# Householder steps in two unequal column blocks, with the side matmuls spread anew

## The chip, the cores and the metric

The kernel runs on one core of a Trainium2 chip. The metric is the device time of one execution in microseconds, the median of the runs. The core has a matrix engine (TensorE, "PE" in the profile, with its weight loads listed as "PEld"), a vector engine (VectorE, "DVE"), a scalar engine (ScalarE, "ACT"), a general engine (GpSimd, "POOL") and DMA queues, of which this kernel uses mainly the one of SyncE ("SP"). Each engine works through its own instructions in order and waits on semaphores for the others.

## The reference

Input `x` is 8 sequences of 512 tokens with 576 features, with one conditioning vector per sequence. Two layers follow one another.

The first rotates part of each token. A matrix `P` (576 x 64) gives an orthonormal basis by a QR factorization, and each sequence gets its own rotation, the exponential of a skew matrix:

```python
U, _ = jnp.linalg.qr(P)                       # 576 x 64
R = expm(A)                                   # A: 64 x 64 skew, from silu(cond) @ W.T + b
z = jnp.einsum('btn,nd->btd', x, U)
x_rot = x + jnp.einsum('btd,nd->btn', jnp.einsum('btd,bde->bte', z, R) - z, U)
```

The second is a transformer block whose shifts, scales and gates come from `silu(cond) @ ada_w + ada_b`. Its attention is over the 16 heads of one token, not over tokens, and is followed by a gelu MLP of width 2304:

```python
x = x + gate_msa * attention(modulate(layernorm(x), shift_msa, scale_msa))
x = x + gate_mlp * mlp(modulate(layernorm(x), shift_mlp, scale_mlp))
```

All is float32.

## The kernel before

The kernel has two parts. A preparation computes the basis, the eight exponentials and the modulations; the main part then runs the block for 16 units of 256 tokens. The change lies in the preparation alone.

**The factorization.** `P` lies in SBUF as `m`: 128 partitions, five row chunks (`NK`), 64 columns (`R`). It is factored by 64 Householder steps, each a call of `qr_step(j, ...)`. In step j:

- TensorE copies row j to all partitions (`rp`, L274) and sums the column products over the partitions with a matrix of ones (`dp`, L282): entry j of `dp` is the squared norm of column j, the others are the inner products with it.
- VectorE takes the sign (`sg`, L291), zeroes the entry of row j in each column's place on the diagonal (`m<-m,off`, L292), and makes the reflected row (`row`, L295). ScalarE takes the root (`nrm`, L298).
- VectorE makes the coefficients `w` (L320) and the divisor `den` and its reciprocal `r` (L323, L335).
- VectorE updates the columns to the right: an outer product `up` (L327), then `m<-up,r,m` (L337), both in two halves of the columns.
- `column_products(j + 1)` makes the products of the next column with all (`pr`, L263) and sums them over the five chunks (`t`, L268). Step j + 1 begins with these.
- `finish` notes the diagonal's value (`av`, L306) and the column's largest entry (`vmax`, L307) and makes what must still be subtracted on the diagonal (`dg`, L310); the returned function subtracts it during the next step (L311).

With fewer than 16 columns left there is one block instead of two halves.

**Beside it.** TensorE has time between `dp` of one step and `rp` of the next. The generator `beside()` fills it: the main loop calls it once after each step from step 2 on, and what it issues stands in TensorE's queue behind that step's `dp` and ahead of the next `rp`. It does four things in turn:

- `skew_entries`: 8 groups of 5 matmuls ("pieces", L405), the entries of the skew matrices; then `skew_rows` sends them through DRAM into `au`.
- `modulations`: 9 groups of 5 matmuls against `ada_w` (L364; a piece here too), each group followed by a ScalarE copy and a load of another block of weights, and four groups followed by a set of small transposing matmuls, `modulation` (L375).
- the series of `expm`: 7 products of 64 x 64 blocks (L429) with additions on GpSimd (L462 to L489), spread over 13 calls.
- 19 squarings: two such products each (`pe` and `pf`), a ScalarE copy of each (L511) and a GpSimd addition for each (L513) that the next squaring reads.

`paced(n, ...)` hands out n pieces a call. In the kernel before, the skew pieces come four a call in steps 4 to 13, the modulations three a call from step 14 on and beside the series (steps 18 to 30), and the squarings in steps 31 to 49 with no other pieces. What is left runs afterwards.

The order of TensorE, VectorE, ScalarE and GpSimd in this part is the order in which the code issues (`manual_schedule`). The order of the loads on SP's queue is made by a planner. Loads for the main part go into memory that the preparation has used and wait until it is free: the first of them (L1048) waits for the last matmul against `ada_w`.

After the last step a serial tail (L574 to L703) forms the triangular factor's inverse by doubling and the matrices `u`, `ut` and `gz`, with which the main part begins.

## Time and profile before

| | us |
|---|---|
| median of 3 runs | 2158.01 |
| lowest and highest of them | 2157.17, 7304.47 |
| the profiled execution, its own time | 2156.77 |
| its span in the profile | 2155.1 |
| start of `sg` in step 0 and in step 63 | 5.87, 213.13 |
| busy over the span: PE, PEld, DVE, ACT, POOL | 2051.7, 1621.1, 1818.1, 432.9, 730.3 |
| mean granted TensorE clock | 0.96 |

The span is the time from the first to the last instruction that the profiler saw; the execution's own time also holds some 1.7 us around it. The highest of the three runs lies far off the other two, and the median is not moved by it. "Granted clock" is the TensorE clock as a share of full speed. A matmul of float32 values appears as two instructions, so a "piece" is two matmul records. A step j is counted from its `sg` to the next one.

### The profile page before, as it was taken

How to read it: one execution, taken by the hardware profiler on the slowest of the kernel's cores; microseconds unless marked ns; L12 is line 12 of the kernel's file. 1: busy time of each engine (PE TensorE's matmuls, PEld its weight loads, DVE VectorE, ACT ScalarE, POOL GpSimd, SP SyncE). 2: the span in 40 equal slices, each digit the busy share in tenths (PEclk: the TensorE clock that was granted, in tenths of full speed). 3: DMA queues.
4: the chain of work that ended last, by engine and by line, in shares of the span. 5: the costliest groups of instructions: out<-in, count | busy, mean ns of one | idle time of the engine just before them, and what ended most of it. 6: DMA issues, size and time to landing. Idle time of an engine off the chain costs nothing.

```text
span 2155.1 us, 28246 instructions
## 1 busy us (share of the span) xinstructions
PE 2051.7 (95%) x10109; PEld 1621.1 (75%) x10109; DVE 1818.1 (84%) x2548; ACT 432.9 (20%) x1040; POOL 730.3 (34%) x959
## 2 busy tenths in 40 slices
PE   5996898999999999999999999999999999998998
PEld 3476666777878878887878787888878787776777
DVE  8898499799997988979797979798997999989821
ACT  2232222221211221222121121121121211111210
POOL 2331153241523333333333243323333434343322
PEclk9855799999999999999999999999999999999999
DMA  8202256375757666575748484756657676665564
GB/s 278 87 2 75 82 189 176 116 227 167 216 192 205 210 185 213 170 236 161 249 137 270 127 266 147 223 194 195 221 177 222 194 226 166 205 188 189 168 193 139
DMA packets 251456, 392.44 MB, mean 182 GB/s; under 512 B 86926, under 2 KB 139099, under 8 KB 251316
## 3 DMA queue, kind: packets, MB, share of 16 engines
q1 hardware_dynamic: 225396, 364.09, 54.9%
q10 hardware_dynamic: 25920, 26.55, 3.6%
q8 instruction: 80, 1.31, 0.2%
q14 instruction: 60, 0.49, 0.1%
HBM read 331.63 MB, written 58.94 MB: 181 GB/s over the span
## 4 chain that ended last, share of the span: by engine, by line
PE 75%; DVE 16%; issue 3%; POOL 2%; DMA 2%; ACT 2%; ACTq 0%; SPq 0%; POOLq 0%; DVEq 0%
PE fc L1001 25%; PE qkvp L821 15%; PE fc L1075 9%; PE fc L1080 6%; PE pj L957 5%; DVE sc L866 3%; PE fc L1077 3%; PE p L1106 2%; DVE qk L859 2%; PE ada L364 1%; PE rot L762 1%; PE zps L751 1%; DVE att L894 1%; DVE pv L887 1%; PE dp L282 1%
## 5 line engine op out<-in xcount | busy, mean ns | idle before, releaser
L1001 PE MATMUL fc<-h2T,w 128*128 128x256 f32 x2304 | 519.0, 381 | 3.4 <-ACT h2T L977 2.3
L821 PE MATMUL qkvp<-wqkv,hT 128*128 128x288 f32 (+1 forms) x1920 | 484.4, 409 | 7.5 <-ACT qs L832 5.3
L1001 PEld LDWEIGHTS fc<-h2T,w 128*128 128x128 f32 x2304 | 433.6, 191 | 70.9 <-ACT h2T L977 9.5
L821 PEld LDWEIGHTS qkvp<-wqkv,hT 128*128 128x128 f32 (+1 forms) x1920 | 363.0, 191 | 110.0 <-ACT qs L832 7.1
L859 DVE TENSOR_TENSOR qk<-qkv 128x2304 f32<-128x2304 f32 x128 | 336.7, 2631 | 4.2 <-ACT qkv L829 2.0
L887 DVE TENSOR_TENSOR pv<-sc,qkv 128x2304 f32<-128x2304 f32 x128 | 333.5, 2606 | 2.7
L894 DVE TENSOR_REDUCE att<-pv 128x144 f32<-128x2304 f32 x128 | 326.0, 2547 | 3.1
L866 DVE TENSOR_REDUCE sc<-qk 128x64 f32<-128x2304 f32 x128 | 326.2, 2548 | 2.5
L1100 POOL TENSOR_TENSOR s<-gt 128x128 f32<-128x128 f32 x144 | 88.9, 619 | 453.3 <-ACT gt L1022 453.3
L1022 ACT ACTIVATE gt<-fc,b 128x256 f32<-128x256 f32 x288 | 118.8, 471 | 610.1 <-PE fc L1001 575.2
L1075 PE MATMUL fc<-wq,gt 128*128 128x288 f32 x576 | 170.8, 417 | 9.9 <-ACT gt L1022 6.7
L1080 PEld LDWEIGHTS fc<-wt,ss 128*128 128x128 f32 x1152 | 161.2, 191 | 15.3
L1080 PE MATMUL fc<-wt,ss 128*128 128x144 f32 x1152 | 165.1, 287 | 0.0
L1033 POOL TENSOR_TENSOR x<-x,mt 128x288 f32<-128x288 f32 x64 | 71.6, 1120 | 227.3 <-DVE mt L1032 227.3
L832 ACT COPY qs<-qkvp 128x288 f32<-128x288 f32 x180 | 71.5, 397 | 378.4 <-PE qkvp L821 337.9
L1097 POOL TENSOR_TENSOR ss<-gt 128x128 f32<-128x128 f32 x144 | 116.9, 812 | 69.6 <-PE fc L1080 68.0
L1099 POOL TENSOR_TENSOR ss<-gt,ss 128x128 f32<-128x128 f32 x144 | 133.0, 924 | 10.0
L1075 PEld LDWEIGHTS fc<-wq,gt 128*128 128x128 f32 x576 | 99.4, 190 | 44.4 <-issue 15.6
L957 PE MATMUL pj<-w2q_p,aT 128*128 128x288 f32 x384 | 104.0, 406 | 2.9 <-DVE u L1137 1.6
L146 POOL TENSOR_TENSOR rstd_m<-rstd_m,mhalf 128x1 f32<-128x1 f32 x32 | 26.7, 835 | 222.1 <-DVE rstd_m L145 222.1
L1075 PE MATMUL fc<-wt,gt 128*128 128x288 f32 x288 | 93.9, 408 | 0.0
L1077 PE MATMUL fc<-wq,ss 128*128 128x288 f32 x288 | 93.9, 408 | 0.0
(265 smaller groups left out, 2379.9 us busy)
## 6 DMA issues: line engine op xcount, KB each, us to landing
w<-in_fc_w SPq DMA_DIRECT2D x288, 256.0 KB, 5.0
wq<-in_fc_q SPq DMA_DIRECT2D x144, 432.0 KB, 4.3
wt<-comb_d SPq DMA_DIRECT2D x144, 432.0 KB, 5.6
tok<-qs ACTq DMA_DIRECT2D x180, 144.0 KB, 1.8
qkv<-tok SPq DMA_DIRECT2D x30, 864.0 KB, 4.6
w2q_p<-in_proj_w SPq DMA_DIRECT2D x32, 432.0 KB, 4.0
xT<-in_x_t SPq DMA_DIRECT2D x16, 640.0 KB, 4.9
w1t<-in_fc_t SPq DMA_DIRECT2D x80, 128.0 KB, 4.4
```

Source lines behind the costliest of these rows:

```text
L821: nc.tensor.matmul(ps, lhsT=hT[0:k, c, i * 128 : (i + 1) * 128], rhs=wqkv[0:k, c, cols], start=c == 0, stop=c == NK - 1,)
L859: nc.vector.tensor_tensor(pr, q[:, c * HC : (c + 1) * HC].unsqueeze(2).to_broadcast([128, HC, H, DH]), k.unsqueeze(1).to_broadcast([128, H ...
L866: nc.vector.tensor_reduce(sc[t][:, c * HC : (c + 1) * HC, :], pr, AX.X, ALU.add)
L887: nc.vector.tensor_tensor(pr, sc[t][:, c * HC : (c + 1) * HC, :].unsqueeze(2).to_broadcast([128, HC, DH, H]), v.unsqueeze(1).to_broadcast( ...
L894: nc.vector.tensor_reduce(att[:, c * HC : (c + 1) * HC, :], pr, AX.X, ALU.add)
L957: nc.tensor.matmul(ps, lhsT=aT[0:k, c, :], rhs=w, start=c == 0, stop=c == NK - 1)
L1001: nc.tensor.matmul(bank[:, k], lhsT=lhs, rhs=h2T[rows, c, 0 : NU * 128], start=start, stop=stop, skip_group_check=True)
L1022: nc.scalar.activation(gt[:, k].rearrange("p t s -> p (t s)"), bank[:, k], AF.Gelu, bias=b1[:, 2 * g + k : 2 * g + k + 1])
L1075: nc.tensor.matmul(p[k], lhsT=whole[k][0], rhs=whole[k][1], start=g == 0, stop=stop)
L1077: nc.tensor.matmul(p[2], lhsT=whole[2][0], rhs=whole[2][1], start=g == 0, stop=stop)
L1080: nc.tensor.matmul(bank[:, side], lhsT=lhs, rhs=rhs[:, n * QUARTER : (n + 1) * QUARTER], start=False, stop=stop, skip_group_check=True,)
L1099: nc.gpsimd.tensor_tensor(ss[:, 2], gt[:, 1, 0], ss[:, 1], ALU.subtract)
```

## The change

The columns are no longer halved. `split(lo)` puts the first quarter of those left in one block and the rest in another (still one block below 16). The two blocks have sums, products and `dp` tiles of their own, and the order within a step becomes: both outer products, `r`, the update of the quarter, `vmax`, the products of the next column with the quarter, the update of the rest, the sums of the quarter, the products and sums of the rest. `w` is made block by block. `av` and, while there are two blocks, `den` are made on ScalarE (`den` as `av` times `nrm`). The signs and diagonal values of all steps are kept in `sgs` and `avs`, and the diagonal is corrected once, after the last step, instead of in every step.

Beside it, the skew pieces come three a call (steps 4 to 16, and one more in 17), the modulation pieces three a call in steps 17 to 21 and two a call beside the series (steps 22 to 34), and none beside the squarings, which are steps 35 to 53. The rest comes one a call from step 54.

```diff
@@ -243,32 +243,33 @@
         vmax = prep.tile([128, R], F32, tag="vmax", name="vmax")
-        def halves(lo):
-            n = R - lo
-            if n < 16:
-                return [(lo, R)]
-            return [(lo, lo + n // 2), (lo + n // 2, R)]
+        avs = prep.tile([128, R], F32, tag="avs", name="avs")
+        sgs = prep.tile([128, R], F32, tag="sgs", name="sgs")
+        def split(lo):
+            first = lo + (R - lo) // 4
+            return [(lo, R)] if R - lo < 16 else [(lo, first), (first, R)]
         def wide(n):
             return [128, NK, n]
-        def column_products(j):
-            t = qrs.tile([128, R], F32, tag="t", name=f"t_{j}")
-            prods = []
-            for h, (a, b) in enumerate(halves(j)):
-                pr = qrs.tile(wide(R), F32, tag=f"pr{h}", name=f"pr_{j}_{h}", bufs=1)
-                nc.vector.tensor_tensor(
-                    pr[:, :, a:b], m[:, :, a:b], m[:, :, j : j + 1].to_broadcast(wide(b - a)), ALU.mult
-                )
-                prods.append(pr)
-            for pr, (a, b) in zip(prods, halves(j)):
-                nc.vector.tensor_reduce(t[:, a:b], pr[:, :, a:b].rearrange("p c i -> p i c"), AX.X, ALU.add)
+        def product(j, k, a, b):
+            pr = qrs.tile(wide(R), F32, tag=f"pr{k}", name=f"pr_{j}_{k}", bufs=1)
+            nc.vector.tensor_tensor(pr[:, :, a:b], m[:, :, a:b], m[:, :, j : j + 1].to_broadcast(wide(b - a)), ALU.mult)
+            return pr
+        def summed(j, k, a, b, pr):
+            t = qrs.tile([128, R], F32, tag=f"t{k}", name=f"t_{j}_{k}")
+            nc.vector.tensor_reduce(t[:, a:b], pr[:, :, a:b].rearrange("p c i -> p i c"), AX.X, ALU.add)
             return t
-        def qr_step(j, t, done):
+        def qr_step(j, ts):
             rp = ps_qr.tile([128, R], F32, tag="rp", name=f"rp_{j}")
             nc.tensor.matmul(
@@ -278,66 +279,75 @@
                 start=True,
                 stop=True,
             )
-            dp = ps_qr.tile([128, R], F32, tag="dp", name=f"dp_{j}")
-            nc.tensor.matmul(dp[:, j:R], lhsT=ones, rhs=t[:, j:R], start=True, stop=True)
-            def small(tag):
-                return qrs.tile([128, 1], F32, tag=tag, name=f"{tag}_{j}")
+            dps = []
+            for k, (t, (a, b)) in enumerate(zip(ts, split(j))):
+                dp = ps_qr.tile([128, R], F32, tag=f"dp{k}", name=f"dp_{j}_{k}")
+                nc.tensor.matmul(dp[:, a:b], lhsT=ones, rhs=t[:, a:b], start=True, stop=True)
+                dps.append(dp)
+            def small(tag, n=1):
+                return qrs.tile([128, n], F32, tag=tag, name=f"{tag}_{j}")
             n = R - j
-            row, sg, nsg, nrm, av = (small(x) if x != "row" else None for x in ("row", "sg", "nsg", "nrm", "av"))
-            row = qrs.tile([128, R], F32, tag="row", name=f"row_{j}")
+            row, nrm, den, r = small("row", R), small("nrm"), small("den"), small("r")
+            sg, av = sgs[:, j : j + 1], avs[:, j : j + 1]
             nc.vector.tensor_scalar(sg, rp[:, j : j + 1], 0.0, -2.0, ALU.is_ge, ALU.mult)
+            nc.vector.scalar_tensor_tensor(
+                row[:, j:R], sg.to_broadcast([128, n]), 1.0, rp[:, j:R], ALU.add, ALU.mult
+            )
             nc.vector.tensor_tensor(
                 m[:, 0, j:R], m[:, 0, j:R], off[:, j : j + 1].to_broadcast([128, n]), ALU.mult
             )
-            nc.vector.scalar_tensor_tensor(
-                row[:, j:R], sg.to_broadcast([128, n]), 1.0, rp[:, j:R], ALU.add, ALU.mult
-            )
-            nc.scalar.activation(nrm, dp[:, j : j + 1], AF.Sqrt, bias=tiny)
-            nc.scalar.activation(nsg, sg, AF.Identity, bias=ones[:, 0:1])
-            if done:
-                done()
-            def finish():
-                dg = small("dg")
-                nc.vector.tensor_scalar(av, nrm, row[:, j : j + 1], None, ALU.subtract)
+            nc.scalar.activation(nrm, dps[0][:, j : j + 1], AF.Sqrt, bias=tiny)
+            nc.scalar.activation(av, row[:, j : j + 1], AF.Identity, bias=nrm, scale=-1.0)
+            def largest():
                 nc.vector.tensor_reduce(
                     vmax[:, j : j + 1], m[:, :, j], AX.X, ALU.max, apply_absolute_value=True
                 )
-                nc.vector.tensor_scalar(dg, ident[:, j : j + 1], av, nsg, ALU.mult, ALU.mult)
-                return lambda: nc.vector.tensor_tensor(
-                    m[:, 0, j : j + 1], m[:, 0, j : j + 1], dg, ALU.subtract
-                )
+            cols = split(j + 1)
+            if len(cols) == 1:
+                largest()
             if j + 1 == R:
-                return None, finish()
-            w = qrs.tile([128, R], F32, tag="w", name=f"w_{j}")
-            den, r = small("den"), small("r")
-            nc.vector.scalar_tensor_tensor(
-                w[:, j + 1 : R], row[:, j + 1 : R], nrm, dp[:, j + 1 : R], ALU.mult, ALU.subtract
-            )
-            nc.vector.tensor_scalar(den, nrm, row[:, j : j + 1], nrm, ALU.subtract, ALU.mult)
-            outer = []
-            for h, (a, b) in enumerate(halves(j + 1)):
-                up = qrs.tile(wide(R), F32, tag=f"up{h}", name=f"up_{j}_{h}", bufs=1)
+                return None
+            if len(cols) == 1:
+                nc.vector.tensor_scalar(den, nrm, row[:, j : j + 1], nrm, ALU.subtract, ALU.mult)
+            else:
+                nc.scalar.activation(den, av, AF.Identity, scale=nrm)
+            w = small("w", R)
+            for dp, (a, b) in zip(dps, split(j)):
+                a = max(a, j + 1)
+                if a < b:
+                    nc.vector.scalar_tensor_tensor(w[:, a:b], row[:, a:b], nrm, dp[:, a:b], ALU.mult, ALU.subtract)
+            def outer(k, a, b):
+                up = qrs.tile(wide(R), F32, tag=f"up{k}", name=f"up_{j}_{k}", bufs=1)
                 nc.vector.tensor_tensor(
                     up[:, :, a:b],
                     m[:, :, j : j + 1].to_broadcast(wide(b - a)),
                     w[:, a:b].unsqueeze(1).to_broadcast(wide(b - a)),
                     ALU.mult,
                 )
-                outer.append(up)
-                if h == 0:
-                    nc.vector.reciprocal(r, den)
-            for up, (a, b) in zip(outer, halves(j + 1)):
-                nc.vector.scalar_tensor_tensor(
-                    m[:, :, a:b], up[:, :, a:b], r, m[:, :, a:b], ALU.mult, ALU.add
-                )
-            return column_products(j + 1), finish()
+                return up
+            def update(up, a, b):
+                nc.vector.scalar_tensor_tensor(m[:, :, a:b], up[:, :, a:b], r, m[:, :, a:b], ALU.mult, ALU.add)
+            ups = [outer(k, *ab) for k, ab in enumerate(cols)]
+            nc.vector.reciprocal(r, den)
+            update(ups[0], *cols[0])
+            if len(cols) == 2:
+                largest()
+            pr = product(j + 1, 0, *cols[0])
+            if len(cols) == 2:
+                update(ups[1], *cols[1])
+            ts = [summed(j + 1, 0, *cols[0], pr)]
+            if len(cols) == 2:
+                ts.append(summed(j + 1, 1, *cols[1], product(j + 1, 1, *cols[1])))
+            return ts
         def paced(n, parts):
@@ -528,14 +538,15 @@
         def beside():
             yield
             yield
-            yield from paced(4, [skew_entries(g) for g in range(8)])
+            yield from paced(3, [skew_entries(g) for g in range(8)])
             skew_rows()
-            rest = paced(3, [modulations()])
-            for _ in range(4):
-                next(rest)
+            rest = modulations()
+            for _ in range(5):
+                for _ in range(3):
+                    next(rest)
                 yield
             for free in expm(*eyes):
-                if free:
+                for _ in range(2 if free else 0):
                     next(rest, None)
                 yield
             for _ in rest:
@@ -551,9 +562,9 @@
         first_xt = xin.tile([128, D], F32, tag="xt", name="xt_0_0", bufs=2)
         eyes = identities()
         side = beside()
-        t, done = column_products(0), None
+        ts = [summed(0, k, a, b, product(0, k, a, b)) for k, (a, b) in enumerate(split(0))]
         for j in range(R):
-            t, done = qr_step(j, t, done)
+            ts = qr_step(j, ts)
             if j > 1:
                 next(side, None)
             if j == 30:
@@ -569,7 +580,10 @@
         if True:
-            done()
+            dg = prep.tile([128, R], F32, tag="dg", name="dg")
+            nc.vector.scalar_tensor_tensor(dg, sgs, 1.0, avs, ALU.add, ALU.mult)
+            nc.vector.tensor_tensor(dg, dg, ident[:, 0:R], ALU.mult)
+            nc.vector.tensor_tensor(m[:, 0, :], m[:, 0, :], dg, ALU.subtract)
             below = ps_ex.tile([R, 1], F32, tag="ex", name="below")
             nc.tensor.matmul(below, lhsT=vmax, rhs=ones[:, 0:1], start=True, stop=True)
             vv = ps_qr.tile([R, R], F32, tag="rp", name="vv")
@@ -618,7 +632,7 @@
                 nc.scalar.copy(vt[:, c * 128 : c * 128 + rows], ps[:, 0:rows])
             vx_chunk(0)
             for c, s in enumerate(LEVELS[1:], 1):
-                p1 = ps_qr.tile([R, R], F32, tag="dp", name=f"p1_{s}")
+                p1 = ps_qr.tile([R, R], F32, tag="dp0", name=f"p1_{s}")
                 nc.tensor.matmul(p1, lhsT=ls[s], rhs=x_, start=True, stop=True)
                 p1s = qrs.tile([R, R], F32, tag="p1s", name=f"p1s_{s}")
                 nc.vector.tensor_copy(p1s, p1)
@@ -663,7 +677,7 @@
             first_zT = prep.tile([R, 128], F32, tag="first_zT", name="first_zT")
             g0 = back(0)
-            zps = ps_qr.tile([R, 128], F32, tag="dp", name="first_z")
+            zps = ps_qr.tile([R, 128], F32, tag="dp0", name="first_z")
             nc.tensor.matmul(zps, lhsT=sneg[:, 0], rhs=vxs, start=True, stop=False)
             nc.tensor.matmul(zps, lhsT=ident[0:R, 0:R], rhs=first_xT[0:R, 0, 0:128], start=False, stop=True)
             nc.scalar.copy(gz[0:R, 0:HALF], g0)
```

## Prediction, made before the changed kernel was run

> **What bounds the kernel now.** I read the chain of waits first, then the factorization step by step.
>
> ```profile
> PE 75%; DVE 16%; issue 3%; POOL 2%; DMA 2%; ACT 2%; ACTq 0%; SPq 0%; POOLq 0%; DVEq 0%
> ```
>
> After 244 us TensorE sets the end and the change touches nothing there, so what the first 214 us gain or lose arrives whole at the end. Next the busy times by stretch, cut at the instants at which a step's `sg` (L291) starts: steps 4-16, 17-21, 22-34, 35-53, 54-62 (steps 0-3 took 5.87 to 21.70; the tail runs from 213.13 to 243.9). Columns: stretch, us; busy (count) of PE, PEld, DVE, ACT, POOL; clock; DMA.
>
> ```profile
> 21.70:66.28 44.58, 36.23 (x152) 15.85 (x151) 42.77 (x236) 8.96 (x35) 0.00 (x0) 1.00 0.67 224
> 66.28:87.77 21.49, 21.05 (x110) 9.28 (x110) 16.83 (x92) 5.27 (x20) 1.57 (x2) 0.76 0.32 92
> 87.77:137.97 50.20, 45.19 (x326) 25.57 (x322) 42.97 (x235) 12.99 (x48) 24.56 (x34) 0.73 0.10 33
> 137.97:191.77 53.80, 49.12 (x544) 44.32 (x543) 51.64 (x320) 19.66 (x68) 20.87 (x30) 0.50 0.14 46
> 191.77:213.13 21.36, 9.93 (x38) 8.93 (x37) 18.17 (x127) 3.98 (x18) 0.00 (x0) 0.50 0.20 75
> ```
>
> VectorE is full in steps 4-16 (3.43 us each) at full clock. From step 18 the clock comes and goes and PE is as full; through the squarings it is at half and both are full. So this is a VectorE chain with a TensorE load tuned to fit beside it. One VectorE step, the end of step 16 (start, duration):
>
> ```profile
> 63.57 0.26 DVE L320 SCALAR_TENSOR_TENSOR w<-row,nrm,dp 128x47 f32<-128x47 f32 x1
> 63.74 0.27 DVE L323 TENSOR_SCALAR den<-nrm,row 128x1 f32<-128x1 f32 x1
> 63.93 0.27 DVE L327 TENSOR_TENSOR up<-m,w 128x115 f32<-128x115 f32 x1
> ...
> 65.77 0.21 DVE L306 TENSOR_SCALAR av<-nrm,row 128x1 f32<-128x1 f32 x1
> 65.89 0.16 DVE L307 TENSOR_REDUCE vmax<-m 128x1 f32<-128x5 f32 x1
> 66.09 0.27 DVE L310 TENSOR_SCALAR dg<-ident,av,nsg 128x1 f32<-128x1 f32 x1
> 66.28 0.15 DVE L291 TENSOR_SCALAR sg<-rp 128x1 f32<-128x1 f32 x1
> ```
>
> An independent instruction starts some 0.09 us before its forerunner ends; a dependent one some 0.03 us after. And what TensorE pays, at half, full and half clock:
>
> ```profile
> 22.01 3.53 PE L405 MATMUL skew<-wr,sc 128*8 128x252 f32 x8
> 26.05 0.81 PE L405 MATMUL skew<-wr,sc 65*8 65x252 f32 x3
> ...
> 119.29 0.64 PE L274 MATMUL rp<-m,ident 128*128 128x34 f32 x2
> 119.73 0.62 PE L282 MATMUL dp<-t,ones 128*128 128x34 f32 x2
> 120.28 1.45 PE L364 MATMUL ada<-aw,sc 128*8 128x384 f32 x2
> ```
>
> A skew piece (two instructions) costs 3.53/4 = 0.88 us at half clock and 0.47 at full; an `ada` piece 1.29 and 0.65. The starts give `rp` 0.39-0.44, `dp` to the next work 0.55; at full clock (25.47, 25.73, 26.05) about 0.22 and 0.36.
>
> **The change, part by part.**
>
> *VectorE.* Gone per step: `av` 0.12, `dg` 0.18, the diagonal subtraction about 0.12, `den` 0.18 (intervals): -0.60, while there are two blocks. Added: a second `w` +0.17; `row` right behind `sg` and `r` right before its use +0.11; the sum of the large block right behind its product (end + 0.03 instead of overlapped) +0.12. Net about -0.2 to -0.35; I take -0.30. Below 16 columns `den` moves ahead of `w`, both behind `nrm`, and what was removed lay in the wait for `dp` there (206.0 to 206.8): 0, at worst +0.03 a step.
>
> *ScalarE* takes `av` and `den`: `row` ends 0.4 after `sg`, two activations of 0.28 end near 1.05, and `r` starts near 1.15. Hidden; if late, 0.1 a step.
>
> *TensorE* gets a third small product a step: `dp0` between `rp` and `dp1`. Before has no such triple. Floor 0 (where PE waits for VectorE anyway), ceiling a whole `rp` to `dp` spacing: 0.22 at full, 0.39 at half clock; I take the ceiling wherever PE is full. `dp1` keeps the place of `dp`, and only `w1` waits for it.
>
> *The side work.* Skew pieces go three a step (steps 4-16) instead of four (4-13), then 15 `ada` pieces in steps 17-21, two a step beside the series (22-34, four steps later), none beside the squarings (35-53), the last ten one a step from 54. The reload of the skew rows took 10.4 us (step 14 to 66.98); now it has five steps, at least 15 us: hidden. Weight loads on SP's queue waited for the last `ada` product (released at 183.4) and landed by about 196; that product now comes in step 63. Then they still have the 30 us tail for some 11 us of transfer: 0, at worst their 11 us.
>
> *What a step then costs.* At full clock VectorE leads: 3.43 - 0.30 = 3.13. At half clock PE leads: 0.39 + 0.39 + 0.56 + 3 x 0.88 = 3.98. So the clock decides, not the VectorE count.
>
> *The clock.* In before it changes on a grid of 3.41 us. At half, windows with side products in some 0.82 or more of them (22.0-25.5, 69.9-73.3, 100.7-104.1) were followed by full clock; 117.8-121.2 with 0.69 (products as above, `rp`/`dp` counted by their columns) was not. At full, four skew pieces with `rp` and `dp` (1.87 + 0.2 of 3.41 = 0.61) kept it; 66.6-70.0 with about 0.40 lost it. Three pieces: at full, one burst of 1.40 + 0.2 to 0.65 of other work = 0.47 to 0.60; at half, 0.72 to 0.85. Both lie inside the open gaps. I take two thirds half clock.
>
> A page of the Trainium skill speaks here: "TensorE: Matmul & The Clock Gate", section "HAM oscillation — how this bites in real kernels", gives as the rule for a full clock that PE must have no idle gap above some 3.4 us. By that rule PE, which never idles so long from step 4 on, stays at full everywhere, and the sum would be about -25 (every step at its VectorE time: -4, -6, -8, -5 in the four middle stretches, -2 elsewhere): 2133. The rows differ: 0.50 throughout 137.97:191.77 with PE busy 49.12 of 53.80. I go by the rows.
>
> Sum, against each stretch of before:
> - steps 0-3, no side work: 4 x -0.30 = -1.2.
> - steps 4-16: two thirds at 3.98, one third at 3.13 = 3.70 x 13 = 48.1 against 44.6: +3.5. (All full: 40.7, -3.9. All half: 51.7, +7.1.)
> - steps 17-21: three `ada` pieces at half are 3.87 us on end, more than a window, so the clock returns after two steps of 1.34 + 3.87 = 5.2; three of 3.1 and about 0.8 for a `mod` piece: 20.5 against 21.5: -1. (All full 15.5, -6; all half 27.8, +6.)
> - steps 22-34 at half: 13 x 1.34 + 22 x 1.29 + 2 x 1.8 (`mod`) + 7 x 0.98 (products of the series) = 56.3; at full VectorE's 3.0 to 3.2 beside the POOL operations, about 42. Two thirds half: 51.5 against 50.2: +1.5.
> - steps 35-53:
>
> ```profile
> 158.81 1.12 PE L429 MATMUL pf<-ex_f,ex_e 64*64 64x64 f32 x16
> 159.72 1.06 PE L429 MATMUL pe<-ex_e,ex_f 64*64 64x64 f32 x16
> 160.71 0.61 PE L274 MATMUL rp<-m,ident 128*128 128x21 f32 x2
> 161.18 0.59 PE L282 MATMUL dp<-t,ones 128*128 128x21 f32 x2
> 161.72 0.59 PE L429 MATMUL pe<-ex_e,ex_f 64*64 64x64 f32 x6
> ```
>
> PE has no gap: 2.91 a step. With `dp0` it is 1.90 + 0.39 + 0.39 + 0.54 = 3.22: 18 x +0.32 = +6. POOL's two additions (0.72 each) stall VectorE's products with two SBUF operands (`m<-m,off` 0.50 instead of 0.18 at 138.04); VectorE's 2.6 stays under 3.22 unless the stall exceeds 0.6.
> - steps 54-62: one `ada` piece (1.29) between `dp` and `rp`, where PE idles 1.3 to 1.4 in before: 0.03 a step, and about 1 for its `mod`: +1.3.
> - tail: three small operations for one on the diagonal: +0.4.
>
> Together +10.5: the profiled execution's 2156.77 becomes 2167.2. The median of the runs is 1.2 above it: **2168**.
>
> **The rivals.**
>
> *Full clock holds (25%).* Three pieces are dense enough. For it: 0.47-0.60 reaches the 0.61 that held. Against it: fewer columns in every window than before. Sum -1.2 - 3.9 - 6 - 8 + 6 + 0.4 = -12.7: 2145.
>
> *Half clock throughout (17%), the slower side.* It decides where no half-clock window passes what is needed, between 0.69 and 0.82: if that is above 0.80, three pieces rarely restore it. Sum -1.2 + 7.1 + 6 + 6 + 6 + 1.3 + 0.4 = +26: 2184. Against it: the bursts of three `ada` pieces.
>
> *The change does nothing net (5%).* The steps shrink by less than 0.30, since the small block's chain waits as before, and the third product hides: 2150 to 2160.
>
> **How the numbers follow.** Mixed clock 50%, 2155 to 2180; the rivals as above; 3% for something unpriced. A no-change measurement of this kernel is told to within about 2%, 43 us: 2115 and 2201 lie outside every case. Faster 0.03, same 0.92, slower 0.05. The range takes in both clock rivals: 2141 to 2188.
>
> **What would show it.** Right: a stretch of steps 4-16 with a clock below 1.00 and steps near 4.0 us; squaring steps at 3.2 with three weight loads ahead of each pair; the `sg` to `sg` interval 3.1 where the clock is full. Wrong: full clock to step 21, or squaring steps at 2.9 or less (`dp0` hidden), or steps at full clock below 2.9 (VectorE saves more). The tail and all after it should keep their lengths.

## The result, and the profile after

The changed kernel takes 2173.52 us (median of 4 runs, 2172.49 to 2174.38), against 2159.45 us for the kernel before beside it (median of 4 runs, of which one lies far off; 45 later runs have the same median and go from 2153.91 to 2165.90). The ratio, taken without that one run, is 1.0069, with a 95% interval of 1.0049 to 1.0088: 14 us slower, under 1%, but clear of zero. The forecast was 2168, in a range of 2141 to 2188.

The profiled executions are 2156.77 us (span 2155.1) and 2174.38 us (span 2172.7). Step 63 begins at 213.13 us in the first and at 222.93 us in the second, so 9.8 of the 17.6 us between the spans are lost in the factorization. The shares of the chain of waits have moved from VectorE to TensorE (before: PE 75%, DVE 16%):

```profile
PE 78%; DVE 11%; DMA 3%; POOL 3%; issue 3%; ACT 1%; ACTq 0%; SPq 0%; POOLq 0%; DVEq 0%
```

The busy times by stretch of the changed kernel, cut as before at the start of `sg` in steps 0, 4, 17, 22, 35, 54 and 63 (stretch, its length; busy of PE, PEld, DVE, ACT, POOL; clock; DMA):

```profile
6.17:21.11 14.94, 6.67 (x24) 5.71 (x24) 14.02 (x62) 3.33 (x12) 8.74 (x37) 1.00 1.05 356
21.11:71.08 49.97, 47.46 (x157) 23.51 (x157) 42.53 (x196) 13.43 (x47) 0.00 (x0) 0.73 0.55 183
71.08:88.79 17.71, 17.22 (x70) 7.41 (x71) 15.40 (x77) 5.69 (x20) 0.73 (x1) 0.90 0.41 113
88.79:139.49 50.70, 46.29 (x260) 25.77 (x259) 40.64 (x197) 16.64 (x56) 19.59 (x27) 0.73 0.18 54
139.49:200.21 60.72, 59.95 (x696) 56.59 (x697) 51.88 (x263) 28.18 (x88) 25.45 (x37) 0.50 0.01 2
200.21:222.93 22.72, 22.67 (x65) 11.69 (x65) 16.60 (x99) 5.80 (x21) 0.60 (x1) 0.50 0.00 1
```

Steps 4-16 lost 5.4 us and steps 35-53 lost 6.9; steps 17-21 gained 3.8. (Steps 35-53 are the squarings of the changed kernel; before, the squarings stood in 31-49.) In both losing stretches PE is busy almost without a gap (47.46 of 49.97, 59.95 of 60.72), at a clock of 0.73 and 0.50; the 0.73 counts the time ahead of 33.6 us, for which no clock is on record, as full. TensorE, not VectorE, sets these steps. Its timeline in steps 11 and 12 (start, duration), with the VectorE instruction that begins the step:

```profile
48.27 0.67 PE L275 MATMUL rp<-m,ident 128*128 128x53 f32 x2
48.73 1.04 PE L285 MATMUL dp<-t,ones 128*128 128x13 f32 x4
48.98 0.16 DVE L295 TENSOR_SCALAR sgs<-rp 128x1 f32<-128x1 f32 x1 [0.46 <-PE rp L275]
...
49.70 2.69 PE L415 MATMUL skew<-wr,sc 128*8 128x252 f32 x6
52.32 0.67 PE L275 MATMUL rp<-m,ident 128*128 128x52 f32 x2
```

From `rp` to `rp` this is 0.46 + 0.97 (two `dp` products, four records) + 2.62 (three skew pieces) = 4.05 us, and VectorE waits 0.46 us for `rp`. Steps 4-6 and 8-13 all look like that. In the squarings one step is the same thing with two products of the exponentials in the place of the skew pieces:

```profile
156.67 1.12 PE L439 MATMUL pf<-ex_f,ex_e 64*64 64x64 f32 x16
157.58 1.06 PE L439 MATMUL pe<-ex_e,ex_f 64*64 64x64 f32 x16
158.57 0.62 PE L275 MATMUL rp<-m,ident 128*128 128x23 f32 x2
159.02 1.02 PE L285 MATMUL dp<-t,ones 128*128 128x5 f32 x4
159.97 0.37 PE L439 MATMUL pe<-ex_e,ex_f 64*64 64x64 f32 x2
```

These starts give 3.30 us a step; before it was 2.91. That holds up to step 48. From step 49 on there is one block and no third product, and the last five squaring steps take 2.76 to 3.07.

### The profile page after: what moved, and what is told of

Read it like the earlier page. It is cut to its first block, busy times and chain, and to the rows that moved or that the text cites. A ratio compares the mean times of both kernels' runs of the same rounds, so it can differ in the third digit from the quotient of the medians.

```text
span 2172.7 us, 28236 instructions
## 1 busy us (share of the span) xinstructions
PE 2090.9 (96%) x10207; PEld 1646.7 (76%) x10207; DVE 1813.0 (83%) x2360; ACT 454.7 (21%) x1088; POOL 727.8 (33%) x959
## 4 chain that ended last, share of the span: by engine, by line
PE 78%; DVE 11%; DMA 3%; POOL 3%; issue 3%; ACT 1%; ACTq 0%; SPq 0%; POOLq 0%; DVEq 0%
PE fc L1015 25%; PE qkvp L835 16%; PE fc L1089 9%; PE pj L971 6%; PE fc L1094 5%; DVE sc L880 3%; PE fc L1091 3%; PE p L1120 2%; DVE qk L873 2%; PE dp L285 2%; PE ada L374 2%; PE rp L275 1%; PE skew L415 1%; PE rot L776 1%; PE zps L765 1%
## 5 line engine op out<-in xcount | busy, mean ns | idle before, releaser
L1089 PE MATMUL fc<-wq,gt 128*128 128x288 f32 x576 | 170.5, 416 | 10.3 <-ACT gt L1036 7.5
L1113 POOL TENSOR_TENSOR ss<-gt,ss 128x128 f32<-128x128 f32 x144 | 121.7, 845 | 10.0
```

The source lines that it names most:

```text
L1089: nc.tensor.matmul(p[k], lhsT=whole[k][0], rhs=whole[k][1], start=g == 0, stop=stop)
L1113: nc.gpsimd.tensor_tensor(ss[:, 2], gt[:, 1, 0], ss[:, 1], ALU.subtract)
```

## The experiments

Stretches in us, each from one profiled execution, and the ratio to the kernel before with its interval where it was timed:

| kernel | 0-3 | 4-16 | 17-21 | 22-34 | 35-53 | 54-62 | sum | ratio |
|---|---|---|---|---|---|---|---|---|
| before | 15.8 | 44.6 | 21.5 | 50.2 | 53.8 | 21.4 | 207.3 | 1 |
| after | 14.9 | 50.0 | 17.7 | 50.7 | 60.7 | 22.7 | 216.8 | 1.0069 (1.0049-1.0088) |
| after, again | 14.8 | 48.3 | 17.7 | 50.8 | 60.7 | 22.7 | 215.0 | 1.0056 (1.0035-1.0077) |
| new steps, old side work | 14.8 | 45.4 | 19.2 | 49.6 | 59.6 | 22.3 | 210.9 | 1.0034 (1.0020-1.0049) |
| old steps, new side work | 15.7 | 45.0 | 16.4 | 47.5 | 55.3 | 22.3 | 202.2 | 0.9988 (0.9980-0.9996) |
| after + discarded piece | 14.8 | 45.5 | 19.2 | 50.7 | 60.7 | 22.7 | 213.6 | 1.0019 (1.0005-1.0032) |
| before + third product | 15.7 | 46.0 | 18.9 | 47.5 | 59.0 | 21.4 | 208.5 | 1.0022 (1.0014-1.0031) |
| after, one joined product | 16.9 | 51.7 | 19.9 | 50.5 | 59.7 | 22.7 | 221.4 | 1.0075 (1.0054-1.0096) |
| lean halves, old side work | 15.7 | 46.4 | 21.7 | 51.2 | 54.3 | 21.5 | 210.7 | 1.0035 (1.0023-1.0047) |
| lean halves, new side work | 15.7 | 47.2 | 17.5 | 43.8 | 56.2 | 22.2 | 202.6 | 0.9990 (0.9983-0.9998) |
| before, nothing beside | 15.8 | 46.3 | 16.8 | 39.9 | 51.0 | 21.4 | 191.2 | one run |
| after, nothing beside | 14.8 | 45.1 | 16.2 | 40.5 | 54.3 | 22.3 | 193.2 | one run |

The clock makes one stretch of one execution uncertain by more than its decimals. Up to step 30 the kernel "before + third product" (described below) is before's, line for line, and yet its steps 4-30 took 99.3 us for 103.1 (46.0 for 44.6 in 4-16, 18.9 for 21.5 in 17-21): its full clock went from 31.7 to 79.5 us, before's from 25.5 to 69.9. Differences of some 3 us in steps 4-34 are therefore no finding by themselves; the readings below go by single steps at a known clock and by the times of many runs.

**One half of the change at a time.** The two halves of the change, the steps and the side work, were put each on the other's kernel. The edit is the body of `beside()`; this is the old side work under the new steps, and the other kernel has the reverse:

```diff
-            yield from paced(3, [skew_entries(g) for g in range(8)])
+            yield from paced(4, [skew_entries(g) for g in range(8)])
...
-            rest = modulations()
-            for _ in range(5):
-                for _ in range(3):
-                    next(rest)
+            rest = paced(3, [modulations()])
+            for _ in range(4):
+                next(rest)
                 yield
             for free in expm(*eyes):
-                for _ in range(2 if free else 0):
+                if free:
                     next(rest, None)
```

> The new Householder steps with the side schedule of the kernel before (four skew pieces a step, three modulation pieces). Theory (clock and third product): steps 5 to 13 at full clock and 3.1 to 3.2 us, so steps 4 to 16 in 41 to 42 us (44.6 before, 50.0 changed); the squarings, now in steps 31 to 49, still 3.29 each, 6 to 7 us above before; the time 2160 to 2166. Rival (the steps themselves are slower, the side schedule is innocent): steps 4 to 16 near 50 us, time 2173 or more.

> The Householder steps of before with the new side schedule. Theory: three pieces lose the full clock for the old steps too, and a half-clock step is 0.39 + 0.56 + 2.64 = 3.6 us, so steps 4 to 16 in 45 to 48 us; the squarings stay at 2.9 each since there is no third product; time 2156 to 2164. Rival (the side schedule costs nothing, the third product and the new order everything): steps 4 to 16 in 44 us or less, time 2155 or less.

Measured: 2167.49 us for the new steps alone, 2156.29 us for the new side work alone; the kernel before took 2159.45 in both comparisons. So the new side work alone does no harm (its upper bound is 0.9996, a hair better than both kernels), the new steps alone cost 0.34%, and together they cost more than the sum of both. The new steps missed their forecast: steps 4-16 took 45.4 us, not 41 to 42, as steps 4 and 5 (4.90 and 4.66 us) came before the clock rose at 30.3 us, and the time is above 2166; the squaring steps are the 3.29 us expected. The other kernel lies at the lower end of its forecast in both numbers.

Where the two halves meet is the clock. Between 26.4 and 64 us the old steps with three pieces had half clock for at most 6.9 us at a time (29.8-33.3, 36.7-43.5, 53.7-60.6); there three pieces come every 3.65 us:

```profile
39.53 0.68 PE L274 MATMUL rp<-m,ident 128*128 128x55 f32 x2
...
43.18 0.57 PE L274 MATMUL rp<-m,ident 128*128 128x54 f32 x2
```

With the new steps the same pieces come every 4.05 us, and half clock lasted from 37.0 to 64.3 us (38.8 to 62.7 in the second profile). That the wider spacing is the reason fits, but it was not tested by itself.

With the old side work the full clock holds through steps 4-16, and there one sees what a new step is worth to VectorE. Its whole queue in one step at full clock, with the product that brings `rp`:

```profile
47.38 0.15 DVE L295 TENSOR_SCALAR sgs<-rp 128x1 f32<-128x1 f32 x1
...
47.57 0.21 DVE L296 SCALAR_TENSOR_TENSOR row<-sgs,rp 128x53 f32<-128x53 f32 x1
47.69 0.21 DVE L299 TENSOR_TENSOR m<-m,off 128x53 f32<-128x53 f32 x1
...
47.88 0.39 DVE L324 SCALAR_TENSOR_TENSOR w<-row,nrm,dp 128x12 f32<-128x12 f32 x2
...
48.31 0.50 DVE L328 TENSOR_TENSOR up<-m,w 128x65 f32<-128x65 f32 x2
48.72 0.16 DVE L340 RECIPROCAL r<-den 128x1 f32<-128x1 f32 x1
48.91 0.29 DVE L337 SCALAR_TENSOR_TENSOR m<-up,r,m 128x65 f32<-128x65 f32 x1
...
49.12 0.15 DVE L306 TENSOR_REDUCE vmax<-m 128x1 f32<-128x5 f32 x1
49.24 0.23 DVE L262 TENSOR_TENSOR pr<-m 128x65 f32<-128x65 f32 x1
49.38 0.42 DVE L337 SCALAR_TENSOR_TENSOR m<-up,r,m 128x195 f32<-128x195 f32 x1
49.71 0.26 DVE L268 TENSOR_REDUCE t<-pr 128x13 f32<-128x65 f32 x1
...
49.89 0.35 DVE L262 TENSOR_TENSOR pr<-m 128x195 f32<-128x195 f32 x1
...
50.27 0.48 DVE L268 TENSOR_REDUCE t<-pr 128x39 f32<-128x195 f32 x1
...
50.67 0.15 DVE L295 TENSOR_SCALAR sgs<-rp 128x1 f32<-128x1 f32 x1
```

VectorE has no gap, and the step (step 11) is 3.29 us. The same step of before, at full clock too, is 3.35; the first instruction of each part:

```profile
46.59 0.15 DVE L291 TENSOR_SCALAR sg<-rp 128x1 f32<-128x1 f32 x1
...
47.10 0.27 DVE L320 SCALAR_TENSOR_TENSOR w<-row,nrm,dp 128x52 f32<-128x52 f32 x1
...
47.47 0.29 DVE L327 TENSOR_TENSOR up<-m,w 128x130 f32<-128x130 f32 x1
...
47.93 0.62 DVE L337 SCALAR_TENSOR_TENSOR m<-up,r,m 128x130 f32<-128x130 f32 x2
...
49.43 0.21 DVE L306 TENSOR_SCALAR av<-nrm,row 128x1 f32<-128x1 f32 x1
...
49.94 0.15 DVE L291 TENSOR_SCALAR sg<-rp 128x1 f32<-128x1 f32 x1
```

From start to start, the difference of 0.06 is made up so:

| part of a step | before | new |
|---|---|---|
| `sg`, `row`, `m<-m,off` (and the diagonal's subtraction) | 0.51 | 0.50 |
| `w` (and `den`) | 0.37 | 0.43 |
| both `up`, and `r` | 0.46 | 0.60 |
| updates, products and sums | 1.50 | 1.64 |
| `av`, `vmax`, `dg` | 0.51 | 0.12 |

What was taken out is worth 0.39 in the last row, 0.20 in the first (the diagonal's subtraction, 46.90 to 47.10) and 0.19 in the second (`den`, 47.28 to 47.47): 0.78. Of this 0.72 comes back: `row` starts 0.19 after `sg` instead of behind an instruction that it doesn't depend on, `r` stands ahead of the update that needs it (0.19 for 0.07), there is a second `w`, and the large block's product and sum wait for each other (0.38 + 0.40). The mean over steps 9-16 is 3.22 for the new order and 3.31 for the old, 0.09 a step.

**Does the load decide the clock?** A fourth skew piece, whose result nothing reads, was added behind every third one of the changed kernel. It is more work on the engine that sets the step.

```diff
                 nc.tensor.matmul(ps, lhsT=sc[0:k, c, :], rhs=wr[0:k, c, cols], start=c == 0, stop=c == NK - 1)
+                done[0] += 1
+                if done[0] % 3 == 0:
+                    spare = ps_x.tile([B, GROUP], F32, tag="vx", name=f"spare_{g}_{c}")
+                    nc.tensor.matmul(spare, lhsT=sc[0:k, c, :], rhs=wr[0:k, c, cols], start=True, stop=True)
                 yield
```

> The changed kernel, with one more matmul after every third skew piece (a repeat into an unused PSUM tile, so four matmuls a step and three of them needed). Theory (the clock decides steps 4 to 16: three pieces are too thin to keep it at full): more work gives shorter steps; the clock is full in most of steps 5 to 16, the steps there are 3.1 to 3.3 us instead of 4.05, the stretch is 41 to 44 us instead of 50.0, and the time is 6 to 9 us below the changed kernel's, 2165 to 2168. Rival (TensorE's load or VectorE's new order makes the 4 us, whatever the clock): the extra 0.9 us at half clock is added, steps 4.9, stretch 62, time 2185.

Measured: 2161.02 us, 12.5 below the changed kernel. With more to do the stretch is shorter, 45.46 for 49.97 us (48.30 in the second profile), since the clock that came at 30.5 us stays until 78.2. The same steps as above, first the stretch, then TensorE's timeline:

```profile
21.05:66.51 45.46, 40.78 (x183) 20.40 (x183) 41.23 (x197) 13.53 (x47) 0.00 (x0) 1.00 0.58 198
```

```profile
49.20 0.59 PE L421 MATMUL spare<-wr,sc 128*8 128x252 f32 x2
49.90 0.42 PE L275 MATMUL rp<-m,ident 128*128 128x52 f32 x2
...
50.86 0.41 PE L285 MATMUL dp<-t,ones 128*128 128x39 f32 x2 [0.33 <-DVE t L268]
51.21 1.44 PE L417 MATMUL skew<-wr,sc 65*8 65x252 f32 x6
```

Now TensorE waits for VectorE (0.33 us for `t`). That three pieces lose the clock under the new steps, and that the lost clock makes the 4.05 us steps, is shown; the rival's 4.9 us a step and 2185 are out. The stretch missed the 41 to 44 us expected, again by steps 4 and 5 (4.90 and 4.79), and the squarings keep their 60.73 us. The whole 12.5 us isn't explained: the 20 runs fall into 12 from 2155.59 to 2162.59 and 8 from 2167.34 to 2175.33, the profiled one (2169.40) is of the second group, and its factorization is only 3.2 us shorter than the changed kernel's.

**The third product.** A product of the same kind, with eight columns and a result that nothing reads, was put behind `dp` in steps 31 to 50 of the kernel before, where the squarings are:

```diff
             nc.tensor.matmul(dp[:, j:R], lhsT=ones, rhs=t[:, j:R], start=True, stop=True)
+            if 31 <= j < 51:
+                spare = ps_x.tile([128, R], F32, tag="spare", name=f"spare_{j}")
+                nc.tensor.matmul(spare[:, 0:8], lhsT=ones, rhs=t[:, j : j + 8], start=True, stop=True)
```

> The kernel before, with a spare product of eight columns right behind dp in steps 31 to 50 alone, whose result nobody reads. Theory (the third small product is what lengthens the squaring steps, by its weight load on a full TensorE): these steps go from 2.9 to 3.2 to 3.3, 18 of them, and the time is 6 to 8 us above before's, 2165 to 2168; everything else as before. Rival (the squaring steps of the change are longer because of VectorE's order beside GpSimd's additions): they stay at 2.9 to 3.0 and the time at 2158 to 2161.

Measured: 2163.62 us for 2159.05, +0.22% or 4.6 us. The added product in one squaring step, on TensorE:

```profile
150.49 0.62 PE L274 MATMUL rp<-m,ident 128*128 128x24 f32 x2
150.94 0.60 PE L282 MATMUL dp<-t,ones 128*128 128x24 f32 x2
151.36 0.57 PE L285 MATMUL spare<-t,ones 128*128 128x8 f32 x2
151.87 1.12 PE L432 MATMUL pf<-ex_f,ex_e 64*64 64x64 f32 x16
```

`dp` is followed 0.42 us later by the spare, and that by the next work after 0.51. The squaring steps become 3.28 us (2.9 before, 3.29 in the changed kernel), and the 19 squarings take 61.9 us for 56.9: +5.0 us by the trace. The step is as forecast, the time is below the 2165 to 2168 expected; the rival's 2.9 to 3.0 us a step is out.

This gives the loss of 6.9 us in steps 35-53 two causes. Steps 35-48 take 40.83 us before, 40.89 in the old steps with the new side work, 45.90 here and 46.07 in the changed kernel: the 5.2 there are this one product. Steps 49-53 take 12.97 before, 14.42 in the old steps with the new side work and 14.65 in the changed kernel, though none of them has a third product: 1.5 to 1.7 come from the new side work, which puts squarings beside steps 50-53, where before had none.

**Can it be joined again?** In the changed kernel both sums were written to one tile and one `dp` product made of it, behind the second sum; all else stays.

```diff
-            dps = []
-            for k, (t, (a, b)) in enumerate(zip(ts, split(j))):
-                dp = ps_qr.tile([128, R], F32, tag=f"dp{k}", name=f"dp_{j}_{k}")
-                nc.tensor.matmul(dp[:, a:b], lhsT=ones, rhs=t[:, a:b], start=True, stop=True)
-                dps.append(dp)
+            dp = ps_qr.tile([128, R], F32, tag="dp0", name=f"dp_{j}")
+            nc.tensor.matmul(dp[:, j:R], lhsT=ones, rhs=ts[0][:, j:R], start=True, stop=True)
+            dps = [dp, dp]
```

> The changed kernel with one product dp over all columns in place of dp0 and dp1 (both blocks' sums in one tile, so that it starts after the last sum). Theory (the third product is paid wherever TensorE is full): squaring steps 2.9 to 3.05 instead of 3.29, 18 of them, -4 to -7; half-clock steps 3.6 instead of 4.05; at full clock the root now waits for the last sum, up to +0.35 a step; time 2162 to 2169. Rival (VectorE's order sets the squaring steps, with GpSimd's additions in its way): squaring steps stay at 3.3 or grow to 3.6 as the root comes later, time 2173 to 2180.

Measured: 2176.10 us, no better, where the theory had 2162 to 2169 and the rival 2173 to 2180. The wait that was taken off TensorE is back on VectorE:

```profile
51.46 0.64 PE L284 MATMUL dp<-t,ones 128*128 128x53 f32 x2 [0.16 <-DVE t L269]
...
52.14 0.26 ACT L301 ACTIVATE nrm<-dp,tiny 128x1 f32<-128x1 f32 x1 [1.87 <-PE dp L284]
...
52.44 0.39 DVE L323 SCALAR_TENSOR_TENSOR w<-row,nrm,dp 128x12 f32<-128x12 f32 x2 [0.57 <-ACT nrm L301]
```

The last sum, `dp`, the root and `w` follow one another, and VectorE stands 0.57 us. The first steps, with nothing beside them, show the price alone: 16.85 us for 14.94, at half speed (`rp` takes the 0.69 us that it takes at half clock). In the squarings a step is now 3.05 to 3.36 us in steps 35-48, with VectorE full: between the `sg` at 164.88 and the next at 168.12 it has no gap, and its `m<-m,off` takes 0.63 us beside a GpSimd addition. So TensorE's third product sets the changed kernel's squaring step, but with one joined product VectorE sets one nearly as long; for this kernel the rival was right.

**Leaving work out of VectorE without the quarter.** Of the change only this was put into the kernel before: `av` and `den` on ScalarE, the diagonal corrected once at the end, `r` behind the second `up`. The halves and the single `dp` stay. It ran with the old side work and with the new.

```diff
-            nc.scalar.activation(nsg, sg, AF.Identity, bias=ones[:, 0:1])
-            if done:
-                done()
+            nc.scalar.activation(av, row[:, j : j + 1], AF.Identity, bias=nrm, scale=-1.0)
...
-                nc.vector.tensor_scalar(av, nrm, row[:, j : j + 1], None, ALU.subtract)
...
-            nc.vector.tensor_scalar(den, nrm, row[:, j : j + 1], nrm, ALU.subtract, ALU.mult)
+            if len(halves(j + 1)) == 1:
+                nc.vector.tensor_scalar(den, nrm, row[:, j : j + 1], nrm, ALU.subtract, ALU.mult)
+            else:
+                nc.scalar.activation(den, av, AF.Identity, scale=nrm)
...
-                if h == 0:
+                if h == len(halves(j + 1)) - 1:
                     nc.vector.reciprocal(r, den)
```

> The steps of before in two halves with one dp, and of the change only what it takes off VectorE: the diagonal's value and (with two halves) the divisor on ScalarE, the diagonal corrected once at the end; side schedule of before. Theory (the change's gain on VectorE is real but is spent on its second w, its dependent pairs and the third product): a step is then the wait for dp and the root (0.86 from the last sum to w at full clock) plus w to the last sum (2.12 at step 16 without den), 2.98 at step 16 and 3.1 at step 10, against 3.25 and 3.40; steps 4 to 16 in 40 to 42 us, squarings 2.9 as before, time 3 to 7 us under before's median: 2152 to 2156. Rival (what was removed lay in that wait anyway): steps as before, 2157 to 2161.

> The same lean steps with the new side schedule (three skew pieces, two beside the series, none beside the squarings). Theory: three pieces lose the full clock here too, and the half-clock step is TensorE's 0.39 + 0.56 + 2.64 = 3.6 or the chain's 3.3; steps 4 to 16 in 43 to 46 us, the later stretches as with the old steps and the new schedule; time 2150 to 2156. Rival (shorter steps are dense enough to hold the clock with three pieces): steps 4 to 16 in 39 to 41 us, time under 2150.

Measured: 2168.13 us with the old side work, a loss of 0.35% where 2152 to 2156 had been expected, though VectorE is busy 36.97 us of steps 4-16 for 42.77. One step of that stretch at full clock:

```profile
51.04 0.65 DVE L270 TENSOR_REDUCE t<-pr 128x26 f32<-128x130 f32 x2
...
52.27 0.26 ACT L301 ACTIVATE nrm<-dp,tiny 128x1 f32<-128x1 f32 x1 [2.05 <-PE dp L284]
...
52.56 0.27 DVE L315 SCALAR_TENSOR_TENSOR w<-row,nrm,dp 128x51 f32<-128x51 f32 x1 [0.50 <-ACT nrm L301]
```

Here too `w` waits 0.50 us for the root, and it starts 0.87 us behind the last sum's end (0.93 in before). So what the change removes from VectorE (`av`, `dg`, the diagonal's subtraction) had stood between the last sum and `w`, in the time that TensorE and ScalarE need for the square root; without it the time is idle. Taking out `den` didn't help either: from `w` to the first update it takes 0.90 us for 0.82, since `up` (0.30 behind `w`) and the update (0.19 behind `r`) now stand right behind what they depend on. From step 8 to step 16 the steps are the old ones to within 0.03 us, as the rival had it. The loss itself is not explained by this: 1.7 us of it are steps 4 and 5, before the clock rose at 31.7 us instead of 25.5, and the rest stays open. With the new side work the kernel took 2157.35 us: nearly the same as the old steps with it, and its steps 4-16, where the clock comes and goes, are longer than theirs (47.2 for 45.0) and longer than the 43 to 46 expected.

**The steps with nothing beside them.** In both kernels the two lines that hand out side work in the main loop were taken out; all of it then runs after step 63, and nothing is left out.

```diff
             ts = qr_step(j, ts)
-            if j > 1:
-                next(side, None)
```

> The changed kernel with all side work after the last Householder step instead of beside the steps (nothing is left out). Theory (VectorE's order is not what makes 4 us): at half clock and without load the steps 5 to 16 are 3.2 to 3.6 us, falling with the columns, and those beside no squarings at 35 to 50 are 2.4 to 2.8; the time is some 60 to 100 us longer as the side work stands alone. Rival (the new order itself takes 4 us at half clock): steps 5 to 16 stay near 4.0.

> The kernel before with all side work moved behind the last step (nothing is left out), beside the same made of the kernel after, whose steps 0-3, 4-16, 17-21, 22-34, 35-53 and 54-62 took 14.79, 45.09, 16.23, 40.46, 54.34 and 22.28 us with nothing beside them, at half clock from about step 4 on. Theory (the new order takes work off VectorE, but that work lay in the wait for the squared norm's product and the root, and the second coefficient product, the dependent pairs and the third small product take its place): with nothing beside them the old steps are hardly longer, within 0.1 us a step of the new ones, 45 to 46.5 in steps 4-16 and 52 to 55 in 35-53; steps 54-62 21.4, as before. Rival (the new order saves its 0.30 a step and the side work alone takes it back): the old steps are longer by 0.2 to 0.3 each, 48 to 49 in steps 4-16 and 58 to 60 in 35-53.

Measured: one run each, 2261.11 us for the new steps and 2253.05 for the old. Only the stretches are of interest here. First the old steps, then the new ones (4-16 and 35-53):

```profile
21.74:68.03 46.29, 17.08 (x54) 13.02 (x53) 42.64 (x236) 5.75 (x26) 0.00 (x0) 1.00 0.56 191
...
124.71:175.72 51.01, 22.75 (x78) 19.04 (x77) 45.41 (x319) 8.41 (x38) 0.00 (x0) 1.00 0.00 1
```

```profile
21.12:66.21 45.09, 21.09 (x79) 18.40 (x79) 42.22 (x196) 11.05 (x39) 0.00 (x0) 1.00 0.58 200
...
122.90:177.24 54.34, 26.36 (x105) 23.86 (x105) 44.80 (x262) 14.38 (x51) 0.00 (x0) 1.00 0.00 1
```

(The clock column shows 1.00 here because no change of it is on record before 200 us; the products, 0.64 to 0.69 us for `rp` in place of 0.42, were at half speed.) In steps 4-16 the new order is 0.09 us a step shorter. Near step 25, with 39 columns left, both take some 3.15 to 3.2; after that the new order is longer, by 0.18 us a step in 35-53. For the new steps alone, steps 5-16 came out as expected (3.22 to 3.63 us), so VectorE's order doesn't make the 4 us; but steps 35-47 took 2.89 to 3.05, not 2.4 to 2.8. For the old steps the rival (48 to 49 us in steps 4-16, 58 to 60 in 35-53) is out; the theory holds for steps 4-16 and 54-62, and in 35-53 the old steps were shorter still than its 52 to 55. Over all steps it is 2.0 us longer with nothing beside it. What it removes has a fixed price, but what it adds has one too (a second `w`, a product, the waits between dependent pairs); which of these grows against the others as the columns get fewer was not taken apart.

**The changed kernel again.** Nothing was edited. The question was whether the 6 us that the profiled executions differ by after the factorization belong to the change.

> The changed kernel itself once more, in more runs, since the profiled execution puts 9.8 us of the difference ahead of step 63 and some 6 us in the main part, which the change doesn't touch. Reading 1 (the main part's share is only the spread between executions of one kernel: the 45 runs of before go from 2154 at a mean granted clock of 0.965 to 2166 at 0.958, and the profiled run of before was a short one): over more runs the changed kernel lies 10 to 12.5 us above before, and its own runs spread as before's do, with the time falling as the mean clock rises. Reading 2 (something of the change reaches the main part): 14 to 18 us in every run, at a clock of 0.951 to 0.952.

Measured: 2172.31 us (6 runs, 2166.84 to 2175.37) against 2160.23, so +12.1 us. That lies within the first reading's bounds, though the interval (7.6 to 16.6 us) doesn't exclude the second's 14, and the times spread over 9 us where the four earlier ones lay within 2. But the mean clock of these runs goes from 0.951 to 0.960 without the time falling with it, so that part of the reading isn't borne out. In this profile steps 4-16 took 48.30 us, 1.7 less than in the first: it had the full clock from 25.2 to 28.6 us and from 32.0 to 38.8, the first only from 33.6 to 37.0, and steps 7 and 8 fell to 3.40 and 3.24.

## Why the prediction was right

The mechanism was right: the clock decides steps 4-16, at half clock TensorE leads, and the third product is paid wherever TensorE is full. The terms that it named add up to the loss ahead of the main part, 10.3 us measured for the 10.5 forecast. That the sum is this close is partly luck: steps 17-21 and the squarings were each off by more than that, and the clock alone moves such stretches by 2 or 3 us from one execution to the next.

- *At half clock TensorE leads with 3.98 us a step* (three skew pieces). Measured 4.05: the two `dp` products take 0.97 to the next work, 0.95 had been reckoned, and `rp` 0.46 for 0.39. With the old steps the same three pieces at half clock took 3.65. So the third product costs 0.40, and 0.39 was the ceiling that the prediction took.
- *Two thirds half clock in steps 4-16.* Measured four fifths of the stretch's time in the first profile: full clock only from 33.6 to 37.0 us and from 64.3 on, and half clock, by the length of the pieces, ahead of 33.6. In the second it was 65%. Hence +5.4 for +3.5, and +3.7 in the second profile. Full clock throughout, the rival at 2145, didn't happen; the discarded piece shows what decides it. (Of the windows from which the prediction worked out its bounds, 66.6-70.0 is 0.40 full only if the pieces alone are counted; all matmuls but `rp` and `dp` fill 0.74 of it.) Nor would it have given what the rival reckoned: at the 3.2 to 3.3 us that VectorE needs, 13 steps are some 42 us, not 40.7, and the two kernels with new steps and a held clock took 45.4 and 45.5 with their fourth piece, steps 4 and 5 of them before the clock rose.
- *VectorE saves 0.30 us a step at full clock.* This term was mis-sized: it measured 0.09 in steps 9-16 at full clock. The prediction's own count was 0.60 gone and 0.40 added, and it then took a value above the difference. Step 11 has 0.78 gone and 0.72 added. Mis-sized most were the dependent pairs, where `row` behind `sg` and `r` behind both `up` cost some 0.3 instead of 0.11, and `w` in two parts, 0.25 instead of 0.17. The 3.43 us that it starts from also holds step 4, at 4.24 before the clock rose; the mean of steps 5-16 is 3.36. The 3.1 us that was named as a sign did come (3.19 and 3.03 in steps 15 and 16), but before's were 3.24 and 3.22 there. The error cost little, because the term applied only where the clock was full.
- *Steps 0-3: -1.2*, four times 0.30. Measured -0.9, but not as four equal parts: step 0 alone gives 0.66, because there `w` had waited 0.81 us for the root, which now comes from the early quarter's sum; steps 1-3 give 0.07 each, at half speed.
- *Steps 17-21: -1.* Measured -3.8. The clock came back during the last skew steps, at 64.3 us, and the bursts of three pieces held it to 84.8, where they had been expected to spend two steps winning it back. Against the 18.9 us that the third-product kernel took with before's code it would be -1.2.
- *Steps 22-34: +1.5.* Measured +0.5. Its own numbers, 51.5 against 50.2, make +1.3.
- *Squarings: 3.22 us a step, 18 times +0.32, +6.* Measured 3.29 and +6.9, the size right by two errors. Only 14 of the 19 squaring steps have a third product (5.2 us at 0.37 each); and the sum left out that before's steps 50-53, with which it compared, had no squarings beside them (1.7 us).
- *Steps 54-62: +1.3*, measured +1.4; *the tail: +0.4*, and its first product, `vv`, comes 10.3 us later (224.90 for 214.60), 0.5 more than step 63 does.
- *"What the first 214 us gain or lose arrives whole at the end."* It arrived with something on top, and what comes after the tail didn't keep its length. The first is a piece of clock: the first group of the attention's projections, in before and after,

```profile
245.51 5.12 PE L821 MATMUL qkvp<-wqkv,hT 128*128 128x288 f32 x20 [1.40 <-ACT hT L798]
```

```profile
255.79 6.61 PE L835 MATMUL qkvp<-wqkv,hT 128*128 128x288 f32 x20 [1.38 <-ACT hT L812]
```

began while the clock was still at half (it came at 258.8 us, before at 244.0): +1.5. The rest of the difference between the profiled spans, some 6 us, comes later, in both profiles of the changed kernel alike. Matched product by product, 2.3 us of it arise between 300 and 605 us and 1.5 behind 1760 us, and in each of these stretches the changed kernel has one half-clock window of 3.4 us more. Another 1.7 arise between 605 and 1160 us, where the profiled before was the shortest of all kernels here. From the first projection to the end before took 1909.6 us, the changed kernel 1916.9 and 1917.2, and the others 1910.6 to 1915.4. So part of it is a short execution of before (2.7 us below its median) and part is clock; why both profiles of the changed kernel have the extra windows stays open. The medians differ by 14.1 and 12.1 us, of which 10 to 12 are accounted for.

The two late streams that were costed at nothing, the reload of the skew rows and the weights behind the last modulation piece, cost nothing that a wait of the trace shows; the skew rows had landed at 82.8 us and TensorE first read them at 92.8. And the clock rule of the Trainium skill that the prediction weighed ("TensorE: Matmul & The Clock Gate", "HAM oscillation — how this bites in real kernels") would have been wrong here: the clock was 0.50 in steps 35-53 with PE busy 59.95 of 60.72 us, and the time is 2173.52, not 2133.

## What to carry to other kernels

Splitting a sum so that its first part is ready early adds an instruction on the engine that reads it; count that where this engine is already full and at the clock it then has (0.40 us a step here), before counting what the other engine saves. Instructions taken off an engine shorten a loop only if nothing else was under way in their time: see which wait follows them, since here `w` waited 0.50 us for the root as soon as they were gone. And side work on TensorE that is thinned out to make room can lose the clock and so the room: here, with the new steps, three pieces a step took longer than four.

## What was not expected of the hardware

- Work that nothing reads made the program faster: 26 more matmul records in steps 4-16 (183 for 157), and the stretch 4.5 us shorter (2.8 against the second profile), with the clock held from 30.5 to 78.2 us.
- Being busy did not bring the clock back. In the changed kernel PE ran without a gap from 37.0 to 64.3 us, three skew pieces and three small products a step, and the clock stayed at 0.50 throughout, and so it did in all squarings.
- The clock pattern isn't the same in two executions of one kernel (ahead of 40 us the changed one had full clock from 33.6 to 37.0 us in the first profile, from 25.2 to 28.6 and from 32.0 to 38.8 in the second), and the factorization moves by 1.8 us with it.
